# A graph-attention and quantile kernel: four engines ordered by hand in the attention, lists loaded one tile ahead, one product per half row of the search

## The chip, the core and the metric

The kernel runs on one core of one Trainium2 chip. A core has engines that work at the same time, each through its own list of instructions in order: TensorE (PE) for matrix products, VectorE (DVE), ScalarE (ACT) and GpSimd (POOL) for elementwise work, and SyncE (SP), which here issues DMA transfers only. ACT and POOL issue transfers too. Instructions of different engines wait for each other by semaphores. The metric is the device time of one execution in microseconds (us), lower is better, given as the median of several runs. A separate execution, recorded by the hardware profiler, gives the views that are read here.

## What is computed

Two graph layers over 4096 nodes with 128 features, both on the same adjacency matrix of integers (4096 x 4096, each entry 1 with chance 1/128, so some 32 neighbours a node). The first layer has eight heads (cut from the reference):

```python
Wh = jnp.einsum('nd,hde->hne', nodes, W)
f1 = jnp.einsum('hnd,hd->hn', Wh, a1)
f2 = jnp.einsum('hnd,hd->hn', Wh, a2)
e = jax.nn.leaky_relu(f1[:, :, None] + f2[:, None, :], negative_slope=ALPHA)
att = jnp.where((adj > 0)[None, :, :], e, jnp.float32(-9000000000000000.0))
att = jax.nn.softmax(att, axis=-1)
h = jax.nn.elu(jnp.einsum('hnm,hmd->hnd', att, Wh))
cat = jnp.transpose(h, (1, 0, 2)).reshape(N, NHEADS * DIM)
out = _layernorm(nodes + jax.nn.elu(cat @ W1 + b1), gamma, beta)
```

The second layer removes some neighbours of each node by their rank in its list, sorts the rest feature by feature, takes the mean of the three quartiles, mixes it with the node's own row, and multiplies by a last matrix:

```python
vals = jnp.where(keep[:, :, None], x[None, :, :], big)
svals = jnp.sort(vals, axis=1)
for q in QUANTILES:
    idx = jnp.maximum(jnp.ceil(q * n_keep).astype(jnp.int32) - 1, 0)
    picked = jnp.take_along_axis(svals, idx[:, None, None], axis=1)[:, 0, :]
    agg = agg + w_q * picked
agg = (1.0 - SELF_RATIO) * agg + SELF_RATIO * x
out = agg @ W.T + b + x
```

## The kernel before

Nodes are handled in tiles of 128, one node per partition, in three blocks of 2, 8 and 22 tiles (`BLOCKS`, L54). A block goes through these steps.

**Search** (`neighbours`, L532). For each tile the adjacency rows come in two halves of 2048 integers (1 MB, issued from ACT, three buffers `adj_t`). ACT turns a half into bf16 signs and counts them (L547). DVE then works in pieces: for 512 columns it multiplies the signs by a falling ramp `back` (L568), so that each entry holds its place in a chunk of 128, and MAX8 (L573) takes the eight largest of each chunk. After both halves, more rounds of MAX8 (L585, L587) pull the neighbour list out of the chunks. The function is a generator: every `yield` is a piece, and a tile has `PIECES` of them.

**Records and order** (`complete_records` L592, `rank_by_count` L652). A record holds a node's list, its number of neighbours, its own index, its scores and its features. The nodes of a block are ranked by their number of neighbours, and POOL scatters the records by rank to a DRAM tensor `recs_d` of that block (L379), one scatter per tile (`scatter`, L193, an indirect DMA). Tiles that are read back then have lists of similar length, so each has a fixed cap (`CAPS`).

**Attention on a sorted tile**, driven by `step` (L342):
- `fetch_rows` (L755) loads the records `R` back from SP (L762). Columns of the list come in layers 32, 32, 16, 8 or 4 wide (`layers`, L75). A layer narrower than 32 puts several nodes' neighbours in a row and loads list and scores again from SP (L771, L775), eight transfers a layer. DVE transposes lists and scores (L791 to L799) to `idx` and `f1x`. Then POOL gathers the neighbours' rows of `xt_d` one column at a time into `G` or, for a short rest, `Gs` (`gather`, L184, an indirect DMA of 128 rows).
- `weigh_rows` (L816), one tile later: DVE and ACT form scores and exponentials `z` (L825 to L827), DVE spreads them to `pf` (L839), PE sums weighted rows in PSUM tiles `y` (L860), ACT copies each `y` to `raw` (L871), DVE divides by the sum (L875 to L878), PE turns and ACT copies to `yT` (L887, L888).
- `transform` (L895), once for every two tiles, or four in the last block: the head matrices, ELU, `W1`, ELU and the layer norm, with the result `x1` (L954 to L974). `step` scatters `x1` to DRAM (L347, named x_d in the profile) at the following call.

`weigh_rows` and `transform` are generators too. `step` advances the weighing by a turn, then the open transform by a turn, then so many pieces of the next block's search; after the search's quota of the step it returns. In the first two blocks DVE, PE and ACT follow exactly this order (`manual_schedule(engines=ORDERED)`, L407), while POOL's order is left to a scheduler. In the last block, where no search is left, all are left to the scheduler. That block also ranks all 4096 nodes, scatters their lists to `all_d` (L397, four tiles a step), and works out kept neighbours and slots from it (`kept_rows`, `slot_places`). Three more calls of `step` (L414) finish the open tiles.

**Sort** (L424 to L470): POOL gathers the kept neighbours' `x1` rows (`vals`), DVE and ACT run a selection network on them (L1129, L1133), and the result is scattered to the output. Here all four engines have a hand order, which the change leaves alone.

Buffers come from pools with a fixed number each. `R` has 5 in the first two blocks and 8 in the last, `idx` and `f1x` 6, `sgn` 2, `y` 4 of one PSUM bank. `G` has 2, and a third in the last block (`take`, L744). A tile that is written waits until the readers of the buffer's earlier use are done.

Of the kernel before, what the change touches and what calls it, by code (L numbers as in the profile page):

```python
# [9 lines left out]
F32 = mybir.dt.float32  # L10
BF16 = mybir.dt.bfloat16
I32 = mybir.dt.int32
# [4 lines left out]
DRAM = bass.MemoryType.DRAM  # L17
ORDERED = {mybir.EngineType.DVE, mybir.EngineType.PE, mybir.EngineType.Activation}
ALL = ORDERED | {mybir.EngineType.Pool}

# [43 lines left out]
TURN = 12  # L64
YBANKS = 4

# [142 lines left out]
def kernel(  # L209
# [132 lines left out]
    def step(fetch=None, pieces=None, quota=0, size=2, more=None):  # L342
        if fetch:
            weigh.append(fetch_rows(tc, pools, narrow[turn[0] % 2], *fetch, xt_d, bad, uses))
            turn[0] += 1
        while store:
            scatter(nc, x1_d, *store.pop(0))  # L347
        if len(weigh) > 1 or (weigh and not fetch):
            R, parts = weigh.pop(0)
            place = len(members)  # L350
            members.append(R)
            turns = len(parts) + 13
            each = -(-quota // turns)
            done = 0
            for _ in weigh_rows(tc, attp, pools, pp, parts, turned, place, size, consts):
                if tails and next(tails[0], True):
                    tails.pop(0)
                for _ in range(min(each, quota - done)):
                    next(pieces, None)
                    done += 1  # L360
            quota -= done
            if len(members) == size:
                tails.append(
                    transform(tc, attp, pp, more, turned.pop(0), list(members), consts, store)
                )
                members.clear()
        elif not fetch:
            while tails:
                if next(tails[0], True):
                    tails.pop(0)  # L370
        for _ in range(quota):
            next(pieces, None)

    t0 = 0
    for b, n in enumerate(BLOCKS):
# [5 lines left out]
        if last:  # L381

            cp.release()
            adjp.release()
            wp = tc.alloc_tile_pool(name="order", bufs=1, side="right")
            cp = tc.alloc_tile_pool(name="cnt_all", bufs=2, side="right", reuse_waits="tile")
            found = rank_by_count(tc, cp, kp, num, jp1, before, oneb, 0, NT)
            ranks = wp.tile([P, NT], I32, name="ranks")
            nc.vector.tensor_copy(ranks, found)
            cp.release()  # L390
            cp = tc.alloc_tile_pool(name="lists", bufs=2, side="right", reuse_waits="tile")
            pools.append(cp)
            waiting = list(range(NT))
            for i in range(n):
                step((recs_d[b], i, CAPS[n][i], t0 + i), size=2 if i in (0, n - 1) else 4, more=kp)
                for t in waiting[:4]:
                    scatter(nc, all_d, rec[:, t, 0:REC1], ranks[:, t : t + 1])  # L397
                waiting = waiting[4:]
                if i == n // 2:
                    R = cp.tile([P, NT, REC1], F32, name="all", bufs=1)  # L400
                    nc.sync.dma_start(R, all_d.rearrange("(t p) w -> p t w", p=P))
                    kept_rows(tc, cp, R, jp1, pidx, idx, own_i, bad, limits)
                    slot_places(tc, cp, R, picks, limits)
        else:
            pieces = search(t0 + n, BLOCKS[b + 1])
            quota = -(-BLOCKS[b + 1] * PIECES // n)
            with tc.manual_schedule(engines=ORDERED):  # L407
                for i in range(n):
                    step((recs_d[b], i, CAPS[n][i], t0 + i), pieces, quota, more=kp)
                for _ in pieces:  # L410
                    pass
        t0 += n
    for _ in range(3):
        step(size=2, more=kp)  # L414
    count_bad(tc, cp, kp, bad, ones, total)
    cp.release()
# [115 lines left out]
def neighbours(tc, adjp, rec, num, adj, tiles, back, chunk):  # L532
# [11 lines left out]
    def sign():  # L544
        t, i, cnt, adj_t = loads.pop(0)
        sgn = adjp.tile([P, half], BF16, name="sgn", bufs=2)
        nc.scalar.activation(sgn, adj_t, AF.Sign, accum_out=cnt[:, i : i + 1])  # L547
# [6 lines left out]
    for _ in range(3):  # L554
        load(*todo.pop(0))
    sign()
    while signs:
        if loads:
# [4 lines left out]
        if i == 0:  # L563
            first = adjp.tile([P, NCH * 8], F32, name="first")
        for b in range(half // 512):

            key = sgn[:, ts(b, 512)].rearrange("p (c w) -> p c w", w=CW)
            nc.vector.tensor_tensor(  # L568
                key, key, back.unsqueeze(1).to_broadcast([P, 512 // CW, CW]), ALU.mult
            )  # L570
            c0 = i * half + b * 512
            for c in range(512 // CW):
                nc.vector.max(first[:, ts(c0 // CW + c, 8)], key[:, c, :])  # L573
            yield
# [17 lines left out]
def complete_records(tc, cp, rec, num_all, bad, jp1, pidx, t0, n):  # L592
# [3 lines left out]
    for a in range(t0, t0 + n, step):  # L596
# [11 lines left out]

        has = tmp("has")
        nc.vector.tensor_scalar(has, keys, 0.0, None, ALU.is_gt)  # L610
# [133 lines left out]
def take(pools, shape, name, turn, bufs=2):  # L744
# [3 lines left out]
    if len(pools) > 1:  # L748
        turn[name] = turn.get(name, 0) + 1
        if name == "R" or (name == "G" and turn[name] % 3 == 0):  # L750
            pool, bufs = pools[1], 8 if name == "R" else 1
    return pool.tile(shape, F32, name=name, bufs=bufs)


def fetch_rows(tc, ap, narrow, rec_d, i, cap, t, xt_d, bad, turn):  # L755

    nc = tc.nc

    R = take(ap, [P, REC], "R", turn, 5)
    rows = rec_d[ts(i, P), :]  # L760
# [19 lines left out]
    parts = []  # L780
    G, col = None, 0
    for s0, w in layers(cap):
        k = P // w
        idx = ap[0].tile([P, 32], I32, name="idx", bufs=6)
        if w == 32:
# [6 lines left out]
        if w < 32 or f1x32 is None:  # L792
# [4 lines left out]
            )  # L797
            f1x = ap[0].tile([P, 32 * H], F32, name="f1x", bufs=6)
            nc.vector.transpose(f1x, f1b.rearrange("p h g -> p (h g)"))  # L799
        if w == 32:  # L800
            f1x32 = f1x
        f1v = f1x.rearrange("p (h g) -> p g h", h=H)[:, 0:w, :]
        if w == 32:
            G, col = take(ap, [P, 32, XW], "G", turn), 0
# [11 lines left out]
def weigh_rows(tc, ap, pools, pp, parts, turned, place, size, consts):  # L816
# [16 lines left out]
    for half in range(2):  # L833
# [13 lines left out]
        for b in range(4):  # L847
            y = pp.tile([P, 512], F32, name="y", bufs=YBANKS)[:, 0 : 2 * (D + 1)]
            yv = y.rearrange("p (a d) -> p a d", a=2)
            for i, ((w, k, G, _), pf) in enumerate(zip(parts, pfs)):  # L850
                both = w == 32 or (w == 16 and split == 1)
                m = max(min(k * H, P) * (2 if both else 1), 32)
                for p0 in range(0, P, m):
# [4 lines left out]
                    else:  # L858
# [35 lines left out]

def transform(tc, ap, pp, more, yT, members, consts, store):  # L895

# [486 lines left out]
```

## Time and profile before

| what | us |
|---|---|
| median of 3 runs | 3860.11 |
| lowest and highest of them | 3859.21, 3861.66 |
| the profiled execution | 4473.73 |
| its span, first to last instruction | 4471.8 |
| DVE busy | 2634.2 |
| POOL busy | 2284.8 |
| ACT busy | 1265.3 |
| PE busy | 815.7 |

The stages of the profiled execution can be told by their transfers. The first search runs until the first records are scattered at 77 us. Block 0's attention and the search of the next 8 tiles take until 325, block 1's attention and the search of the last 22 tiles until 1101, where the records of the last block begin to be scattered. The last block gathers until 2412, its tail ends near 2487, where the sort's gathers begin, and the sort runs to the end.

A table of windows gives, for each stretch, the busy time and instructions of each engine. Busy time counts only what an engine does; POOL's issue of an indirect transfer counts[...], and the pause between two of them does not. A list of waits gives, for an engine and line, what its idle time waited for, in total, how often and at the longest. "issue" means that the profile shows nothing it waited for, "remote" a releaser that it can't name. A timeline line is one instruction or a run of equal ones: start, busy time, engine, line, operation and tiles, and in brackets the idle time before it with its releaser. The profiled execution is longer than the timed ones, so its times are not those of a timed run one by one.

### The profile page before, as it was taken

To read this page: it belongs to the slowest core of one execution; us is meant where nothing else is said; L and a number is where in the kernel's file an instruction comes from. 1 tells how busy PE (TensorE), PEld (TensorE's weight loads), DVE (VectorE), ACT (ScalarE), POOL (GpSimd) and SP (SyncE) were. 2 spreads that over 40 slices of the span, in tenths; PEclk is the share of its full clock that TensorE was granted. 3 is DMA by queue.
4 is the path that set the end of the run, shared out by engine and by line. 5 is a ranking of instruction groups with operands and counts; after the bars stand their busy time and mean duration, and the time that the engine had idled before them with its cause. 6 is when DMAs were issued, how large, how long until landed. Compare 5 with 4: busy or idle time off the path is not lost. (4 is left out here: it accounts for less than half of the span.)

```text
span 4471.8 us, 18412 instructions
## 1 busy us (share of the span) xinstructions
PE 815.7 (18%) x2751; PEld 469.4 (10%) x2753; DVE 2634.2 (59%) x5147; ACT 1265.3 (28%) x2352; POOL 2284.8 (51%) x2452
## 2 busy tenths in 40 slices
PE   2001212223231413332425110000000001000101
PEld 1000110111121201111112000000000000000001
DVE  5665667767111205110212436888878999999897
ACT  2112222222010213121213213333333444443433
POOL 1332343454657465756663575666565334455530
PEclk9955555555565656655656555555555555555555
DMA  5313333231222121212221111111111001111110
GB/s 168 105 48 111 97 101 96 91 93 43 54 46 53 36 57 41 55 47 48 48 51 28 40 53 39 47 45 47 40 45 41 22 21 30 31 38 35 36 28 3
DMA packets 115233, 241.18 MB, mean 54 GB/s; under 512 B 51904, under 2 KB 68288, under 8 KB 106912
## 3 DMA queue, kind: packets, MB, share of 16 engines
q0 software_dynamic: 76224, 161.01, 14.2%
q10 hardware_dynamic: 12160, 68.49, 4.5%
q1 hardware_dynamic: 26720, 10.41, 1.2%
q14 instruction: 103, 0.84, 0.1%
q8 instruction: 26, 0.43, 0.0%
HBM read 228.56 MB, written 11.18 MB: 54 GB/s over the span
## 5 line engine op out<-in xcount | busy, mean ns | idle before, releaser
L1133 DVE TENSOR_TENSOR vals<-low,vals 128x1024 f32<-128x1024 f32 (+9 forms) x1359 | 1403.0, 1058 | 338.9 <-ACT low L1129 129.8
L185 POOL DMA_INDIRECT G<-xt_d,idx x1092 | 1060.0, 971 | 736.3 <-issue 480.8
L185 POOL DMA_INDIRECT vals<-x_d,idx x960 | 911.9, 950 | 295.4 <-issue 287.5
L1129 ACT COPY low<-vals 128x1024 f32<-128x1024 f32 (+10 forms) x701 | 607.4, 876 | 968.6 <-DVE vals L1133 621.1
L871 ACT COPY raw<-y 32x129 f32<-32x129 f32 (+1 forms) x928 | 239.2, 258 | 854.6 <-remote 516.9
L860 PE MATMUL y<-G,pf 128*64 128x258 f32 (+1 forms) x1200 | 289.9, 518 | 978.3 <-issue 574.9
L1143 PE MATMUL st_ps<-ident,u 128*128 128x128 f32 x344 | 87.1, 437 | 1781.4 <-ACT u L1142 1377.9
L194 POOL DMA_INDIRECT out_dram<-o,own_i x32 | 31.8, 992 | 626.0 <-ACT o L1155 623.7
L875 DVE TENSOR_SCALAR rden<-raw 128x8 f32<-128x8 f32 x32 | 6.2, 194 | 550.5 <-ACT raw L871 407.0
L573 DVE MAX8 first<-sgn 128x8 f32<-128x128 bf16 x1024 | 223.9, 281 | 152.4 <-remote 121.5
L1143 PEld LDWEIGHTS st_ps<-ident,u 128*128 128x128 f32 x344 | 76.0, 327 | 1792.3 <-ACT u L1142 1385.4
L860 PEld LDWEIGHTS y<-G,pf 128*64 128x64 f32 (+1 forms) x1200 | 141.5, 191 | 1111.7 <-issue 861.6
L547 ACT ACTIVATE sgn<-adj_t 128x2048 bf16<-128x2048 int32 x64 | 122.1, 1907 | 303.0 <-DVE first L573 177.0
L908 DVE TENSOR_SCALAR e<-e 128x512 f32<-128x512 f32 x64 | 28.0, 437 | 242.4 <-ACT e L935 131.8
L194 POOL DMA_INDIRECT x_d<-x,R x32 | 32.9, 1027 | 260.2 <-DVE x L974 235.6
L888 ACT COPY yT<-turned 128x512 f32<-128x512 f32 x64 | 65.6, 1026 | 302.6 <-PE turned L887 157.2
L839 DVE TENSOR_TENSOR pf<-z,own 128x512 f32<-128x512 f32 x124 | 80.6, 683 | 112.1 <-issue 87.5
L887 PE MATMUL turned<-ident,raw 128*128 128x128 f32 x256 | 68.6, 420 | 391.6 <-DVE raw L878 233.1
L916 PE MATMUL o<-hv,W_sb 128*128 128x256 f32 (+1 forms) x176 | 93.8, 650 | 229.6 <-DVE hv L910 118.5
L1133 DVE TENSOR_TENSOR most<-low,most 128x1024 f32<-128x1024 f32 (+7 forms) x116 | 131.9, 1167 | 2.6 <-issue 0.5
L185 POOL DMA_INDIRECT Gs<-xt_d,idx x92 | 89.6, 974 | 85.7 <-remote 30.0
L585 DVE MAX8 rec<-first 128x8 f32<-128x256 f32 x256 | 109.3, 427 | 35.8 <-remote 18.7
(180 smaller groups left out, 1774.7 us busy)
## 6 DMA issues: line engine op xcount, KB each, us to landing
adj_t<-in_adj_dram ACTq DMA_DIRECT2D x64, 1024.0 KB
G<-xt_d,idx POOLq DMA_INDIRECT x1092
vals<-x_d,idx POOLq DMA_INDIRECT x960
R<-rec_d SPq DMA_DIRECT2D x128, 26.4 KB
xt_d<-rec SPq DMA_DIRECT2D x4, 548.0 KB
score<-rec_d SPq DMA_DIRECT2D x132, 1.0 KB
rec<-in_x_dram SPq DMA_DIRECT2D x4, 512.0 KB
Gs<-xt_d,idx POOLq DMA_INDIRECT x92
```

Of the source, the lines that this page charges most:

```text
L185: nc.gpsimd.indirect_dma_start(out=dst, out_offset=None, in_=rows, in_offset=bass.IndirectOffsetOnAxis(ap=idx, axis=0),)
L547: nc.scalar.activation(sgn, adj_t, AF.Sign, accum_out=cnt[:, i : i + 1])
L573: nc.vector.max(first[:, ts(c0 // CW + c, 8)], key[:, c, :])
L585: nc.vector.max(top, first)
L839: nc.vector.tensor_tensor(pf.rearrange("p (g k h) -> p g k h", g=g2, k=k), z[:, ts(half, g2), :].unsqueeze(2).to_broadcast(spread), own[w] ...
L860: nc.tensor.matmul(yv[p0 : p0 + m], lhsT=pf[:, c : c + m], rhs=rhs, start=(i == 0), stop=(i == len(parts) - 1), skip_group_check=True,)
L871: nc.scalar.copy(raw[p0 : p0 + m, 4 * half + b, :], yv[p0 : p0 + m, a, :])
L887: nc.tensor.transpose(t_ps[:, b, :], yn[:, 4 * half + b, :], ident)
L916: nc.tensor.matmul(o, lhsT=consts["W1_sb"][:, h, :], rhs=hv[:, ts(j, n)], start=(h == 0), stop=(h == H - 1),)
L1129: nc.scalar.copy(kept, low)
L1133: nc.vector.tensor_tensor(high if end else low, kept, high, ALU.max if end else ALU.min)
L1143: nc.tensor.matmul(st_ps, lhsT=u, rhs=ident, start=(i == 0), stop=(i == len(terms) - 1))
```

## The change

- All four engines (POOL too) follow a hand order in the attention of all three blocks; the three closing steps and the count of bad rows are moved into the last block's ordered region. `ORDERED` goes.
- `fetch_rows` is split. `list_rows` (the loads from SP and DVE's transposes) runs one tile ahead: tile i+1's before the step of tile i, so at the start of a block two tiles' lists come first. `R` goes to 7 and 9 buffers, `idx` and `f1x` to 9.
- The search multiplies a half row by `back` in one instruction of 2048 instead of four of 512. `sgn` has 3 buffers and two signs are made ahead.
- `y` becomes a tile of two banks, with 2 buffers; ACT copies two blocks at once, so 928 copies of 32x129 become 464 of 32x258, and a tile's weighing has four turns fewer. A transform of four tiles takes more turns than one weighing has then and ends in the next tile's, so its `x1` is scattered one step later. `x1` gets a tile of its own in another pool.
- A temporary of `complete_records` shares a buffer.

In the last block the written order makes POOL issue, step by step, a tile's gathers, then the `x1` scatters that are due (two or four), then four `all_d` scatters. All 22 record scatters come ahead of them.

```diff
...
         if fetch:
-            weigh.append(fetch_rows(tc, pools, narrow[turn[0] % 2], *fetch, xt_d, bad, uses))
-            turn[0] += 1
+            weigh.append(fetch_rows(tc, pools, fetch, xt_d, uses))
         while store:
...
             members.append(R)
-            turns = len(parts) + 13
+            turns = len(parts) + 9
             each = -(-quota // turns)
...
                 tails.append(
-                    transform(tc, attp, pp, more, turned.pop(0), list(members), consts, store)
+                    transform(tc, attp, pools[0 if size == 2 else -1], pp, more, turned.pop(0), list(members), consts, store)
                 )
...
             next(pieces, None)
+
+    def lists(b, i):
+        turn[0] += 1
+        t = sum(BLOCKS[:b]) + i
+        cap = CAPS[BLOCKS[b]][i]
+        return list_rows(tc, pools, narrow[turn[0] % 2], recs_d[b], i, cap, t, bad, uses)
...
             waiting = list(range(NT))
-            for i in range(n):
-                step((recs_d[b], i, CAPS[n][i], t0 + i), size=2 if i in (0, n - 1) else 4, more=kp)
-                for t in waiting[:4]:
-                    scatter(nc, all_d, rec[:, t, 0:REC1], ranks[:, t : t + 1])
-                waiting = waiting[4:]
-                if i == n // 2:
-                    R = cp.tile([P, NT, REC1], F32, name="all", bufs=1)
-                    nc.sync.dma_start(R, all_d.rearrange("(t p) w -> p t w", p=P))
-                    kept_rows(tc, cp, R, jp1, pidx, idx, own_i, bad, limits)
-                    slot_places(tc, cp, R, picks, limits)
+            with tc.manual_schedule(engines=ALL):
+                ready = [lists(b, 0)]
+                for i in range(n):
+                    if i + 1 < n:
+                        ready.append(lists(b, i + 1))
+                    step(ready.pop(0), size=2 if i in (0, n - 1) else 4, more=kp)
+                    for t in waiting[:4]:
+                        scatter(nc, all_d, rec[:, t, 0:REC1], ranks[:, t : t + 1])
+                    waiting = waiting[4:]
+                    if i == n // 2:
+                        R = cp.tile([P, NT, REC1], F32, name="all", bufs=1)
+                        nc.sync.dma_start(R, all_d.rearrange("(t p) w -> p t w", p=P))
+                        kept_rows(tc, cp, R, jp1, pidx, idx, own_i, bad, limits)
+                        slot_places(tc, cp, R, picks, limits)
+                for _ in range(3):
+                    step(size=2, more=kp)
+                count_bad(tc, cp, kp, bad, ones, total)
         else:
...
             quota = -(-BLOCKS[b + 1] * PIECES // n)
-            with tc.manual_schedule(engines=ORDERED):
+            with tc.manual_schedule(engines=ALL):
+                ready = [lists(b, 0)]
                 for i in range(n):
-                    step((recs_d[b], i, CAPS[n][i], t0 + i), pieces, quota, more=kp)
+                    if i + 1 < n:
+                        ready.append(lists(b, i + 1))
+                    step(ready.pop(0), pieces, quota, more=kp)
                 for _ in pieces:
...
         t0 += n
-    for _ in range(3):
-        step(size=2, more=kp)
-    count_bad(tc, cp, kp, bad, ones, total)
     cp.release()
...
         t, i, cnt, adj_t = loads.pop(0)
-        sgn = adjp.tile([P, half], BF16, name="sgn", bufs=2)
+        sgn = adjp.tile([P, half], BF16, name="sgn", bufs=3)
         nc.scalar.activation(sgn, adj_t, AF.Sign, accum_out=cnt[:, i : i + 1])
...
     sign()
+    if loads:
+        sign()
     while signs:
...
             first = adjp.tile([P, NCH * 8], F32, name="first")
+        key = sgn.rearrange("p (c w) -> p c w", w=CW)
+        nc.vector.tensor_tensor(
+            key, key, back.unsqueeze(1).to_broadcast([P, half // CW, CW]), ALU.mult
+        )
         for b in range(half // 512):
...
-            key = sgn[:, ts(b, 512)].rearrange("p (c w) -> p c w", w=CW)
-            nc.vector.tensor_tensor(
-                key, key, back.unsqueeze(1).to_broadcast([P, 512 // CW, CW]), ALU.mult
-            )
             c0 = i * half + b * 512
             for c in range(512 // CW):
-                nc.vector.max(first[:, ts(c0 // CW + c, 8)], key[:, c, :])
+                nc.vector.max(first[:, ts(c0 // CW + c, 8)], key[:, b * (512 // CW) + c, :])
             yield
...
-        has = tmp("has")
+        has = tmp("c")
         nc.vector.tensor_scalar(has, keys, 0.0, None, ALU.is_gt)
...
         if name == "R" or (name == "G" and turn[name] % 3 == 0):
-            pool, bufs = pools[1], 8 if name == "R" else 1
+            pool, bufs = pools[1], 9 if name == "R" else 1
     return pool.tile(shape, F32, name=name, bufs=bufs)
...
-def fetch_rows(tc, ap, narrow, rec_d, i, cap, t, xt_d, bad, turn):
-
-    nc = tc.nc
-
-    R = take(ap, [P, REC], "R", turn, 5)
+def list_rows(tc, ap, narrow, rec_d, i, cap, t, bad, turn):
+
+    nc = tc.nc
+
+    R = take(ap, [P, REC], "R", turn, 7)
     rows = rec_d[ts(i, P), :]
...
     parts = []
-    G, col = None, 0
     for s0, w in layers(cap):
-        k = P // w
-        idx = ap[0].tile([P, 32], I32, name="idx", bufs=6)
+        idx = ap[0].tile([P, 32], I32, name="idx", bufs=9)
         if w == 32:
...
             )
-            f1x = ap[0].tile([P, 32 * H], F32, name="f1x", bufs=6)
+            f1x = ap[0].tile([P, 32 * H], F32, name="f1x", bufs=9)
             nc.vector.transpose(f1x, f1b.rearrange("p h g -> p (h g)"))
...
         f1v = f1x.rearrange("p (h g) -> p g h", h=H)[:, 0:w, :]
+        parts.append((s0, w, idx, f1v))
+    return R, cap, parts
+
+
+def fetch_rows(tc, ap, lists, xt_d, turn):
+
+
+    nc = tc.nc
+    R, cap, todo = lists
+    parts = []
+    G, col = None, 0
+    for s0, w, idx, f1v in todo:
+        k = P // w
         if w == 32:
...
         for b in range(4):
-            y = pp.tile([P, 512], F32, name="y", bufs=YBANKS)[:, 0 : 2 * (D + 1)]
-            yv = y.rearrange("p (a d) -> p a d", a=2)
+            if b % 2 == 0:
+                y = pp.tile([P, 2, 512], F32, name="y", bufs=2)
+            yv = y[:, b % 2, 0 : 2 * (D + 1)].rearrange("p (a d) -> p a d", a=2)
             for i, ((w, k, G, _), pf) in enumerate(zip(parts, pfs)):
...
                     )
+            if b % 2 == 0:
+                continue
             m = P // (2 * split)
             for p0 in range(0, P, m):
-                a = p0 // m % 2
-                nc.scalar.copy(raw[p0 : p0 + m, 4 * half + b, :], yv[p0 : p0 + m, a, :])
+                a = p0 // m % 2 * (D + 1)
+                nc.scalar.copy(
+                    raw[p0 : p0 + m, 4 * half + b - 1 : 4 * half + b + 1, :],
+                    y[p0 : p0 + m, :, a : a + D + 1],
+                )
             yield
...
-def transform(tc, ap, pp, more, yT, members, consts, store):
+def transform(tc, ap, own, pp, more, yT, members, consts, store):
...
     yield
-    x1 = ap.tile([P, 4, D], F32, name="x1", bufs=1)[:, 0:m, :]
+    x1 = own.tile([P, m, D], F32, name=f"x1_{m}", bufs=1)
     stats = ap.tile([P, 4, 6], F32, name="stats")
```

More of the change, by code (lines that the diff above doesn't have):

```diff
@@ L17 @@
 DRAM = bass.MemoryType.DRAM
-ORDERED = {mybir.EngineType.DVE, mybir.EngineType.PE, mybir.EngineType.Activation}
-ALL = ORDERED | {mybir.EngineType.Pool}
+ALL = {
+    mybir.EngineType.DVE,
+    mybir.EngineType.PE,
+    mybir.EngineType.Activation,
+    mybir.EngineType.Pool,
+}
 P = 128
@@ L64 @@
 TURN = 12
-YBANKS = 4
 R_NUM, R_OWN, R_F1 = L, L + 1, L + 2
```

## The prediction

> **What bounds the kernel now.** I read the span first, then a table of busy time by stage (cut where the record scatters, the last gather and the sort begin), then the waits of the engine that is busiest in each stage, and last single stretches of the timeline. Columns of the table: stage, length, busy us (instructions) of PE, weight loads, DVE, ACT, POOL, then clock and DMA.
>
> ```profile
> 77.00:325.00 248.00, 17.94 (x58) 7.49 (x59) 159.90 (x593) 38.79 (x64) 97.50 (x102) 0.79 0.32 88
> 325.00:1101.00 776.00, 180.82 (x593) 99.82 (x595) 505.96 (x1788) 192.15 (x393) 321.61 (x324) 0.57 0.30 91
> 1101.00:2412.00 1311.00, 402.63 (x1287) 196.56 (x1285) 255.47 (x668) 246.32 (x735) 820.12 (x848) 0.60 0.21 48
> ```
>
> To be seen: while blocks 0 and 1 run, DVE is the busiest engine (it does the neighbour search); in the last block (third row) DVE has 255 us of work in 1311 and POOL has 820 plus its dispatch. So a saving on DVE counts before 1101 us only, a saving or a loss on POOL after it only.
>
> POOL's row understates it. In the last block it issues gathers like this, and scatters to one DRAM tensor behind each other like the first four lines (start, duration, idle before and its releaser):
>
> ```profile
> 1165.92 0.96 POOL L194 DMA_INDIRECT all_d<-rec,ranks  x1 [0.30 <-issue]
> 1168.39 0.96 POOL L194 DMA_INDIRECT all_d<-rec,ranks  x1 [1.51 <-DMA all_d<-rec,ranks]
> 1171.01 0.95 POOL L194 DMA_INDIRECT all_d<-rec,ranks  x1 [1.66 <-DMA all_d<-rec,ranks]
> 1173.47 0.96 POOL L194 DMA_INDIRECT all_d<-rec,ranks  x1 [1.51 <-DMA all_d<-rec,ranks]
> 1174.74 0.97 POOL L185 DMA_INDIRECT G<-xt_d,idx  x1 [0.30 <-issue]
> 1176.02 0.96 POOL L185 DMA_INDIRECT G<-xt_d,idx  x1 [0.30 <-issue]
> ```
>
> A gather takes 1.25 us from start to start (2405.01 to 2411.25: five in 6.24). A scatter behind a scatter takes 2.52 (1165.92 to 1173.47: three in 7.55), 1.27 more, because it waits until the one before has landed; a single one between gathers takes 1.27 in all.
>
> What stands idle in the two stages beside that (engine, what waited, for whom: us, times, longest):
>
> ```profile
> DVE first L573 <- remote: 121.5, 28, 5.9
> DVE bad L776 <- DMA R<-rec_d: 42.5, 2, 25.4
> DVE z L825 <- DMA G<-xt_d,idx: 34.3, 3, 19.7
> ...
> DVE idx L791 <- DMA list<-rec_d: 7.7, 4, 2.9
> ```
>
> ```profile
> POOL G L185 <- issue: 247.7, 702, 16.3
> POOL x_d L194 <- DVE x L974: 53.3, 2, 44.1
> POOL G L185 <- PE y L860: 47.0, 3, 17.0
> POOL Gs L185 <- remote: 29.7, 3, 16.3
> POOL Gs L185 <- PE y L860: 29.5, 2, 18.3
> ```
>
> Without the 0.30 that belongs to each dispatch, POOL's idle in the last block adds to about 211 us. **The choice that decides this forecast is how much of it exists in a timed run.** The profiled execution took 4473.7 us (span 4471.8), 612 more than the median 3860.1. Much of its idle has no cause that it shows: DVE's own MAX8 waits 4.3 us (121.5/28) behind a product of the same engine. Floor: up to 1101, DVE's "remote" and "issue" waits sum to about 190, leaving 911. The last block without POOL's idle is 1311 - 211 = 1100; its tail 75. The sort (2487 to 4472) is 1985; DVE waits 129.8 there for ACT's copy L1129, 94.8 on "issue" and 30.2 on "remote", leaving 1730. Sum 3816: 44 us under the median, where 656 us of such idle were taken out. So a timed run seems to hold at most about 44 of the last block's 211, by an even share 14. I take 25.
>
> [...] 128x1024 bf16 in 0.68 us, 128x1920 in 1.15. [...] L568 takes 0.41 us for 512 where the fp32 L839 takes 0.68[...].
>
> **The change part by part.**
>
> One product per half row. A piece (product of 512 and four MAX8) repeats every 1.23 us: products start at 800.03 and 801.26. A half row is four, 4.94. After: one product of 2048, by the two bf16 rows above 1.15 + 128 x 0.525 ns = 1.21, plus 16 MAX8 at 0.193 to 0.212, 3.1: 4.33. Saved 0.61 x 60 half rows = 37 us on DVE while it bounds (the first four half rows lie in the opening search, which waits for loads). It also cuts product-to-MAX8 waits from 256 to 64; should a share of the 121.5 us be real (44/656 of it, three quarters gone), 6 more. Together -43; bounds -20 and -90. A third `sgn` buffer and the second sign ahead mean a load is issued after an earlier sign: one load in flight less, +3 in the opening (bounds 0 and +6), nothing later, where a half row comes every 15 us or slower[...].
>
> Lists one tile ahead. What goes: DVE's list waits, 7.7, and the later of the two `R` waits, 17 (42.5 - 25.4), of which I take 10. What comes: at the start of a block SP issues tile 1's lists before tile 0 is weighed, 28 issues at 0.30 to 0.42 for a tile with three narrow layers, +9 at block 1, where the first `R` wait of 25.4 stays. Net -1.
>
> The border to the last block. Before, the last tile of block 1 is weighed around 1098.58, where DVE waits 7.6 us for its gathers and the first record scatter stands behind two x1 scatters that end at 1101; its last needed rank stood at 1089.66. After, that weigh is ordered behind the lists of tiles 0 and 1 and the record scatters start earlier: -8. But the first gather of the last block writes a `G` that this weigh still reads. Before, from first record scatter to first gather: 1101.3 to 1174.7, 73.4, with 17 of the 32 all_d scatters in the waits between record scatters. After: 22 record scatters alone, 62; lists of tile 0 from SP, then of tile 1, about 11 each (1167.2 to 1175.5), and the DVE transposes behind them; then z, exp, pf and the matmuls, 13.6 as at 1098.6 to 1112.2: about 101. +27 on POOL (bounds +10 and +40).
>
> Scatters in bunches. By POOL's order after, all_d goes in fours behind each tile's gathers and x1 in fours or twos before: 35 scatters have a scatter to the same tensor ahead. 35 x 1.27 = 45. Besides, 17 all_d and 2 x1 scatters leave the shadow of the record scatters, where they cost nothing: 19 x 1.26 = 24. +69, less what falls where POOL would wait for a buffer anyway (bounds +40 and +80).
>
> POOL, PE, ACT and DVE by hand in the last block. The number of gathers, 776, is the same: 969 us at 1.25 cannot be ordered away. What can go is idle: -25 as chosen, bounds 0 and -211. The x1 scatters one tile later take away the 44.1 wait for `x`; in that count already. The `R` buffers (9) let a list load wait for an x1 scatter two steps back; three `G` buffers cover it, 0.
>
> Copies of two blocks at once. ACT: 928 copies at 0.268 become 464 at about 0.38 (0.258 plus 129 elements at 0.87 ns, from 128x512 in 0.596 and 128x128 in 0.263): -70 on ACT, which is busy 246 of 1311 us. Nothing, hidden by POOL's gathers; a `y` freed later costs PE a block, hidden too. Uncovered it would be up to 1 us a half tile. The sort is untouched: 0.
>
> Sum: -43 + 3 - 1 - 8 + 27 + 69 - 25 = +22. Most of the profiled excess should come again, so the sum is laid on the median: 3860 + 22 = 3882.
>
> **The rivals.** (1) The idle is real: if the sort and the search hold none of it and gathers run quicker unprofiled, the last block could lose 100 or more. Hand order then removes the waits for `x` (53.3), for `y` (76.5) and remote (29.7). It turns the result once more than 47 us go. With 110: 3860 + 47 - 110 = 3797. For it: the same waits end after PE's `y` on buffers, a plain cause. Against: the floor of 3816. (2) The bunches fall into existing waits: half of the 69 and 12 of the 27 vanish: 3882 - 46 = 3836, also faster. (3) Even: product and idle weigh against the border and bunches, about 3860. (4) The product of 2048 loses the double rate: 2048 x 1.04 ns + 0.15 = 2.3 us (fp32 rows: 512 in 0.68, 1024 in 1.21), 1.1 more each, so 0.49 lost instead of 0.61 saved, 66 us worse: 3948. Against: the 512 row keeps it with the same kind of view.
>
> **How the numbers follow.** A median of this kernel can be told from no change at about 0.2%, 8 us. Forecast 0.43; rival 1 0.26; rival 2 0.18; even 0.10; rival 4 0.03. Faster 0.44, same 0.10, slower 0.46. The predicted time is that of the likeliest case, 3882; its own range, with product -20 to -50, bunches 40 to 80, border 10 to 40 and idle 0 to 44, is 3850 to 3925. To hold 8 in 10 it reaches to rivals 1 and 2: 3790 to 3925.
>
> **What would show it.** Product: 64 rows of 128x2048 near 1.2 us, and the record scatters of the last block starting some 50 us earlier. Border: about 100 us from first record scatter to first gather instead of 73. Bunches: all_d in fours 2.5 us apart. If between the first and the last gather POOL's idle falls far below 211 and the timed run falls with it, the floor was wrong; if it falls and the time doesn't, the idle was the profile's. It is wrong altogether if POOL shows new waits for `R`, `idx` or `G` inside the stream.

## The result and the profile after

The changed kernel takes 3893.8 us (median of 4 runs, 3892.2 to 3897.4), the kernel before 3860.0 beside it: a ratio of 1.0089, 95% interval 1.0075 to 1.0103. It is slower by 34 us, where 22 were forecast.

The profile of the kernel before that the prediction reads (4473.7 us), and the first group of experiments below, are from executions in which the unchanged kernel takes some 4400 to 4470 us instead of 3860. Each group of experiments ran on one chip, a different one each time, and all executions of the unchanged kernel in a group lie at one level: 23 near 4435 in the first, 25 and 7 near 3860 in the others. So times are compared only within a group, or by their ratios to the kernel before. The profile after lies at the usual level (span 3893.3), and a second profile of the kernel before was taken there (span 3853.1, the run `e10_before_again`). These two can be set side by side.

Busy time by stage of the kernel after, in the columns of the prediction's table. The cuts are again the first record scatters of blocks 0, 1 and 2, and the last gather:

```profile
74.60:256.90 182.30, 18.62 (x58) 7.69 (x59) 152.74 (x552) 34.35 (x46) 103.70 (x102) 0.83 0.44 122
256.90:814.00 557.10, 167.53 (x574) 94.85 (x575) 479.20 (x1637) 173.28 (x271) 343.05 (x322) 0.60 0.41 126
814.00:2021.10 1207.10, 376.61 (x1375) 197.59 (x1375) 285.90 (x700) 215.89 (x465) 825.64 (x850) 0.62 0.23 52
```

The same of the kernel before, second profile:

```profile
76.50:263.30 186.80, 18.16 (x59) 7.44 (x59) 158.72 (x596) 38.79 (x64) 99.45 (x103) 0.82 0.41 117
263.30:873.45 610.15, 176.27 (x595) 98.97 (x596) 506.17 (x1786) 191.98 (x393) 323.83 (x325) 0.60 0.37 115
873.45:1984.80 1111.35, 398.86 (x1372) 204.38 (x1370) 273.74 (x703) 264.39 (x778) 826.53 (x848) 0.65 0.22 57
```

To be seen: the two search stages are 57.6 us shorter (4.5 and 53.1), and the last block is 95.8 longer with the same POOL work (825.6 against 826.5 busy). So POOL waits more.

POOL's waits from the first to the last gather of the last block, before (second profile), then from its first record scatter on, after:

```profile
POOL G L185 <- issue: 206.7, 678, 0.3
POOL Gs L185 <- issue: 17.7, 58, 0.3
POOL G L185 <- DMA G<-xt_d,idx: 6.1, 20, 0.3
POOL x_d L194 <- issue: 5.4, 14, 1.4
...
POOL x_d L194 <- DVE wt L1103: 1.7, 1, 1.7
```

```profile
POOL G L188 <- issue: 213.2, 694, 1.4
POOL all_d L197 <- DMA all_d<-rec,ranks: 38.1, 24, 2.7
POOL rec_d L197 <- DMA rec_d<-rec,ranks: 37.5, 20, 2.4
POOL G L188 <- PE y L889: 35.9, 5, 34.6
...
POOL x_d L197 <- DMA x_d<-x,R: 12.9, 8, 1.9
```

Before, every wait in this stream is the 0.3 of a dispatch, but for a few of under 2 us (3.7 us in all beyond the dispatches): there is next to no idle that an order could remove. After, one gather waits 34.6 us, and 24 `all_d` scatters wait for the one ahead to land. On the timeline 14 `x1` scatters stand directly behind another and wait as long; the list gives the scatter ahead as the cause for 8 of them only. Beyond the 0.30 of a dispatch these 38 waits sum to 52.3 us. A bunch of each kind, and that gather, on POOL's timeline:

```profile
945.40 0.96 POOL L197 DMA_INDIRECT all_d<-rec,ranks  x1 [0.30 <-issue]
947.84 0.96 POOL L197 DMA_INDIRECT all_d<-rec,ranks  x1 [1.48 <-DMA all_d<-rec,ranks]
950.31 0.96 POOL L197 DMA_INDIRECT all_d<-rec,ranks  x1 [1.52 <-DMA all_d<-rec,ranks]
952.76 0.96 POOL L197 DMA_INDIRECT all_d<-rec,ranks  x1 [1.49 <-DMA all_d<-rec,ranks]
...
1276.94 1.00 POOL L197 DMA_INDIRECT x_d<-x,R  x1 [0.30 <-issue]
1279.47 0.97 POOL L197 DMA_INDIRECT x_d<-x,R  x1 [1.53 <-DMA x_d<-x,R]
1282.75 1.00 POOL L197 DMA_INDIRECT x_d<-x,R  x1 [2.31 <-DMA R<-rec_d]
1285.59 1.40 POOL L197 DMA_INDIRECT x_d<-x,R  x1 [1.84 <-DMA x_d<-x,R]
```

```profile
910.82 0.97 POOL L188 DMA_INDIRECT G<-xt_d,idx  x1 [34.65 <-PE y L889]
```

The last record scatter starts at 875.22. On DVE meanwhile (kernel after) the lists of tiles 0 and 1 come first, and the weighing whose `G` is wanted starts only at 899.40:

```profile
881.07 0.15 DVE L793 TENSOR_SCALAR bad<-R 128x1 f32<-128x1 f32 x1 [51.39 <-DMA R<-rec_d]
...
889.42 0.15 DVE L793 TENSOR_SCALAR bad<-R 128x1 f32<-128x1 f32 x1 [1.28 <-DMA R<-rec_d]
...
899.40 0.59 DVE L853 TENSOR_TENSOR z<-G,f1x 128x256 f32<-128x256 f32 x1
```

The stages of all kernels, worked out from POOL's timelines (us): when the last block's first record scatter starts, and from there how long it is to the first gather, from that to the end of the last gather, to the sort's first gather, and to the end. The column of gathers holds 776 gathers in every kernel, and the scatters between them: 808 transfers in all before, 828 after.

| kernel | record scatters | to first gather | gathers | tail | sort | span |
|---|---|---|---|---|---|---|
| before, second profile | 873.5 | 73.9 | 1037.5 | 43.2 | 1825.0 | 3853.1 |
| after | 814.0 | 96.8 | 1110.3 | 47.3 | 1824.9 | 3893.3 |
| after less before | -59.4 | +22.9 | +72.8 | +4.1 | -0.1 | +40.2 |
| e9_product_again | 842.9 | 72.3 | 1036.2 | 43.2 | 1825.7 | 3820.3 |
| e5_after_again | 814.7 | 98.1 | 1111.8 | 46.8 | 1825.9 | 3897.3 |
| e6_border | 851.1 | 78.5 | 1106.1 | 47.0 | 1825.4 | 3908.0 |
| e7_singles | 815.3 | 98.4 | 1058.8 | 48.5 | 1825.4 | 3846.3 |
| e8_all_three | 861.6 | 74.6 | 1045.4 | 48.7 | 1825.3 | 3855.6 |
| e11_ordered_border | 809.5 | 71.7 | 1057.6 | 48.0 | 1824.9 | 3811.8 |
| e12_ordered_all | 812.0 | 69.3 | 1051.2 | 47.6 | 1825.8 | 3805.8 |
| first group: e1_before_again | 1083.3 | 74.5 | 1197.1 | 75.6 | 1977.0 | 4407.5 |
| e2_product_only | 976.6 | 73.9 | 1219.4 | 75.6 | 1978.1 | 4323.6 |
| e3_after_four_products | 1098.7 | 99.1 | 1201.2 | 83.8 | 1978.9 | 4461.7 |
| e4_copies_only | 1085.9 | 75.7 | 1195.0 | 84.0 | 1977.5 | 4418.2 |

The profiled executions are 40.2 apart, the medians 34 (39 in the second group below); single executions scatter by a few us.

### The profile page after: what moved, and what is told of

The parts are those of the page before. It is cut to its first block, busy times and chain, and to the rows that moved or that the text cites. A ratio compares the mean times of both kernels' runs of the same rounds, so it can differ in the third digit from the quotient of the medians.

```text
span 3893.3 us, 17676 instructions
## 1 busy us (share of the span) xinstructions
PE 747.3 (19%) x2751; PEld 449.7 (12%) x2753; DVE 2621.1 (67%) x4955; ACT 1196.5 (31%) x1888; POOL 2317.4 (60%) x2452
## 5 line engine op out<-in xcount | busy, mean ns | idle before, releaser
L188 POOL DMA_INDIRECT G<-xt_d,idx x1092 | 1092.0, 1000 | 510.2 <-issue 323.3
L889 PE MATMUL y<-G,pf 128*64 128x258 f32 (+1 forms) x1200 | 255.7, 492 | 907.7 <-DVE pf L867 867.1
L853 DVE TENSOR_TENSOR z<-G,f1x 128x256 f32<-128x256 f32 (+3 forms) x46 | 22.1, 479 | 463.6 <-DMA G<-xt_d,idx 461.6
L855 ACT ACTIVATE z<-z 128x256 f32<-128x256 f32 (+3 forms) x62 | 20.4, 330 | 878.9 <-DVE z L854 877.7
L902 ACT COPY raw<-y 32x258 f32<-32x258 f32 (+1 forms) x464 | 169.7, 366 | 252.8 <-PE y L889 217.2
L590 DVE MAX8 first<-sgn 128x8 f32<-128x128 bf16 x1024 | 208.1, 277 | 2.0
L1167 DVE TENSOR_TENSOR vals<-vals 128x256 f32<-128x256 f32 (+2 forms) x335 | 119.0, 411 | 0.0
L950 PE MATMUL o<-hv,W_sb 128*128 128x256 f32 (+1 forms) x176 | 81.6, 579 | 187.7 <-DVE hv L944 187.7
L197 POOL DMA_INDIRECT rec_d<-rec,ranks x32 | 31.2, 976 | 129.5 <-DVE rec L528 67.2
```

Of the source, the lines that this page charges most:

```text
L188: nc.gpsimd.indirect_dma_start(out=dst, out_offset=None, in_=rows, in_offset=bass.IndirectOffsetOnAxis(ap=idx, axis=0),)
L197: return nc.gpsimd.indirect_dma_start(out=rows, out_offset=bass.IndirectOffsetOnAxis(ap=idx, axis=0), in_=src, in_offset=None,)
L590: nc.vector.max(first[:, ts(c0 // CW + c, 8)], key[:, b * (512 // CW) + c, :])
L889: nc.tensor.matmul(yv[p0 : p0 + m], lhsT=pf[:, c : c + m], rhs=rhs, start=(i == 0), stop=(i == len(parts) - 1), skip_group_check=True,)
L902: nc.scalar.copy(raw[p0 : p0 + m, 4 * half + b - 1 : 4 * half + b + 1, :], y[p0 : p0 + m, :, a : a + D + 1],)
L950: nc.tensor.matmul(o, lhsT=consts["W1_sb"][:, h, :], rhs=hv[:, ts(j, n)], start=(h == 0), stop=(h == H - 1),)
```

## The experiments

The theory is that of the prediction: the product and the lists save time while DVE bounds; the border and the bunches lose it on POOL, which has little or nothing to give in the last block. The rivals: the idle of the last block is real, so that the hand order removes it (the first of the prediction) or the bunches fall into it (the second); the product is hidden, or takes 2.3 us instead of 1.21.

**First group: parts alone.** The kernel before takes 4434.8 us in it.

Unchanged, for a profile (`e1_before_again`):

> The kernel before, unchanged, for a second profile. My theory: the 612 us that its first profile had above the median were the profile's own, so a fresh profile near 3860 us has its stages as follows: record scatters of the last block begin near 860 (the changed kernel: 814), first gather about 73 us later, last gather near 2000, sort about 1825 long as in the changed kernel, and POOL idle in the last block under 45 us. Rival (the idle is real): the record scatters begin earlier than 840 and over 60 us of POOL idle that no scatter explains stand between the first and the last gather. If the profile is again near 4470, neither is told apart.

4409.4 us: at the longer level again, so nothing is told apart. POOL still has long waits in its gathers there (`Gs` for PE's `y` up to 18.4 us), and the stretch takes 1197.1 instead of 1037.5.

Product alone (`e2_product_only`), in the kernel before:

```diff
-        for b in range(half // 512):
-            key = sgn[:, ts(b, 512)].rearrange("p (c w) -> p c w", w=CW)
-            nc.vector.tensor_tensor(key, key, back...to_broadcast([P, 512 // CW, CW]), ALU.mult)
+        key = sgn.rearrange("p (c w) -> p c w", w=CW)
+        nc.vector.tensor_tensor(key, key, back...to_broadcast([P, half // CW, CW]), ALU.mult)
+        for b in range(half // 512):
```

> The kernel before with one product of 2048 per half row, all else as before. My theory: DVE bounds up to the last block, so 60 half rows save 0.61 us each and 0 to 6 us of waits: -37 to -43, 3817 to 3823. Rival A: the product is hidden by other waits, 3850 to 3860. Rival B: the product loses the double rate, about 3888.

4320.5 us, ratio 0.9749 (0.9718 to 0.9779): 114 us, three times the expectation. A product of 2048 takes 1.209 us here, not the 2.3 that rival B means. The two profiles, 83.9 us apart, show where it comes from. MAX8 of the kernel before, then with one product (busy, mean ns, idle before and its releasers):

```profile
L573 DVE MAX8 first<-sgn 128x8 f32<-128x128 bf16 x1024 | 223.8, 281 | 143.4 <-remote 97.0 <-issue 35.6 <-DVE sgn L568 4.1
```

```profile
L573 DVE MAX8 first<-sgn 128x8 f32<-128x128 bf16 x1024 | 209.7, 278 | 22.8 <-issue 12.2 <-remote 5.7 <-DVE sgn L566 3.1
```

At this level the idle before MAX8 falls by 120.6 us with one product; at the usual level the same group has 7.9 us of idle before the change, and no more can go. So the 114 don't carry over.

The changed kernel with four products (`e3_after_four_products`; the edit is the reverse of the one above):

> The changed kernel with four products of 512 per half row again, all else changed. My theory: 37 to 43 us slower than the changed kernel's 3894, 3931 to 3937, if DVE bounds the search there too. Rival: in the changed kernel POOL's gathers of block 1 end no earlier than DVE's ranks, so part of the product's gain is lost already: 3905 to 3920.

4463.8 us, 1.0083 (1.0051 to 1.0115) of the kernel before. The changed kernel itself isn't in this group, so the size asked for stays open. What the table shows: the wait at the border is there again (99.1 against 74.5), while the gathers take only 4.1 us longer than in `e1_before_again`. By POOL's timelines 38 scatters in bunches wait 54.7 us beyond their dispatches there, and the waits ahead of gathers fall from 143.7 to 91.0. So at the level where POOL has idle in its stream, its loss pays for the bunches. Whether the bunches fall into it, as the second rival said, or the hand order removes it, as the first said, isn't told apart.

Copies of two blocks alone (`e4_copies_only`), in the kernel before:

```diff
-            y = pp.tile([P, 512], F32, name="y", bufs=YBANKS)[:, 0 : 2 * (D + 1)]
+            if b % 2 == 0:
+                y = pp.tile([P, 2, 512], F32, name="y", bufs=2)
...
-                nc.scalar.copy(raw[p0 : p0 + m, 4 * half + b, :], yv[p0 : p0 + m, a, :])
+                nc.scalar.copy(raw[p0 : p0 + m, 4 * half + b - 1 : 4 * half + b + 1, :], y[p0 : p0 + m, :, a : a + D + 1])
```

> The kernel before with y in tiles of two banks and ACT's copies of two blocks at once, all else as before (the weighing has as many turns as before). My theory: ACT is not the bound in any stage, 3855 to 3862. Rival: the later release of y or the later end of a weighing holds DVE in block 1 or POOL in the last block: 3865 to 3885; or the fewer ACT instructions free DVE, 3835 to 3850.

4424.4 us, 0.9984 (0.9969 to 0.9998), next to nothing, as said. A copy of 32x258 takes 365 ns in the kernel after, one of 32x129 takes 257 in the kernel before.

**Second group: the border and the bunches in the changed kernel.** The kernel before takes 3860.3 us here, and the changed one first, as the reference (`e5_after_again`):

> The changed kernel once more, as the reference of this group. If the kernel before runs near 3860 here: 3885 to 3900. If it runs near 4435 as in the last group, there the change's product is worth 114 us instead of 37 and the changed kernel should be faster than before: 4464 - 114 to 4464 - 60, 4350 to 4404, with the same costs of border and bunches in it.

3899.0 us, 1.0102 (1.0085 to 1.0119).

The border (`e6_border`):

```diff
             with tc.manual_schedule(engines=ALL):
+                step(size=2, more=kp)
                 ready = [lists(b, 0)]
```

> The changed kernel, but in the last block the last tile of block 1 is weighed ahead of the lists of tiles 0 and 1 instead of behind them. My theory: the first gather no longer waits for the G of that tile and follows the record scatters by about 12 us instead of 35: -20 to -27 against the changed kernel, about the same on either kind of chip. Rival: POOL gets ahead and waits as long for G later in the stream, or the weighing moved forward delays the lists: 0 to -5.

3908.6 us, 10 slower than the changed kernel: a miss. The wait before the first gather did go (78.5 from the first record scatter instead of 98.1), but the record scatters themselves start 36 us later. The weighing came ahead of the last search tile and of the ranks on DVE: the ranking isn't part of the hand-ordered region, and the scheduler put it behind the weighing's start. DVE then sits on the gathers, and POOL on the ranks:

```profile
827.62 0.60 DVE L854 TENSOR_TENSOR z<-G,f1x 128x256 f32<-128x256 f32 x1 [26.65 <-DMA G<-xt_d,idx]
```

```profile
851.12 0.96 POOL L197 DMA_INDIRECT rec_d<-rec,ranks  x1 [10.72 <-DVE ranks L734]
```

Single scatters (`e7_singles`); `between` holds the step's four `all_d` scatters and the `x1` scatters that are due:

```diff
         for g in range(w):
             gather(nc, G[:, col + g, :], xt_d, idx[:, g : g + 1])
+            if g % 3 == 2 and between:
+                scatter(nc, *between.pop(0))
...
-                    for t in waiting[:4]:
-                        scatter(nc, all_d, rec[:, t, 0:REC1], ranks[:, t : t + 1])
```

> The changed kernel, but in the last block all_d and x1 scatters go one by one behind every third gather instead of in fours and twos. My theory: each scatter that had one of its tensor ahead saves 1.27 us, 32 or so of them: -35 to -45 against the changed kernel. Rival (the bunches fall where POOL would wait for G anyway, as PE or DVE set its pace): -10 or less, with new waits for y in their place.

3846.7 us, 52 less than the changed kernel, and 0.9964 (0.9951 to 0.9976) of the kernel before. That is more than the 35 to 45 expected, and what the 38 waits of the kernel after sum to. The gathers take 1058.8 us instead of 1110.3 to 1111.8, and no new wait for `y` comes. The rival falls. POOL's timeline of it; behind the first gather one scatter waits 1.1 us, and no other longer than a dispatch:

```profile
922.01 0.94 POOL L188 DMA_INDIRECT G<-xt_d,idx  x1 [0.30 <-issue]
923.26 1.00 POOL L197 DMA_INDIRECT all_d<-rec,ranks  x1 [0.30 <-issue]
924.56 0.96 POOL L188 DMA_INDIRECT G<-xt_d,idx  x1 [0.31 <-issue]
```

Both, with eight `all_d` scatters between the last eight record scatters (`e8_all_three`). The block's ranks are first copied to a tile that outlives their pool:

```diff
+                for i in range(14, n):
+                    scatter(nc, all_d, rec[:, waiting[0], 0:REC1], ranks[:, waiting[0] : waiting[0] + 1])
+                    waiting.pop(0)
+                    scatter(nc, recs_d[b], rec[:, t0 + i, :], held_i[:, i : i + 1])
```

> The changed kernel with both: the border mended, single scatters, and besides eight of the all_d scatters put between the last eight record scatters, where those wait anyway. My theory: -24 - 40 - 10 = -65 to -85 against the changed kernel, so faster than both kernels: 3810 to 3830 where the kernel before takes 3860. Rival: POOL's gain is eaten by waits for G (PE y), -20 to -40.

3853.2 us, 46 less than the changed kernel but 7 more than with single scatters alone. Neither account: no wait for `G` took the gain. The failure of `e6_border` is in it, with the first record scatter at 861.6, where POOL had waited 33.7 us for a copy of the ranks.

**Third group.** The kernel before takes 3857.7 us.

Product alone again (`e9_product_again`):

> The kernel before with one product of 2048 per half row, once more, for a chip on which the kernel before takes 3860. My theory: -37 to -43 there, 3817 to 3823; its profile shows record scatters of the last block from about 820 and POOL idle in the last block, beside the 0.30 of each dispatch and scatter waits, under 45 us. Rival (the product is worth what it was in the slower group, 114 us): 3746. Rival (most of it is hidden): 3850 or more.

3828.1 us, 0.9925 (0.9908 to 0.9941): 29.6 us, less than the 37 to 43 expected. The record scatters start 30.6 us earlier than before (842.9, not 820), and everything behind them is as it was.

The kernel before again (`e10_before_again`):

> The kernel before for a second profile, on a chip where it takes 3860. My theory: record scatters of the last block from about 860, first gather 73 us later, last gather near 1985, POOL's idle in the last block under 45 us where the first profile had 211. Rival: idle over 60 us there, so that the hand order did remove something.

3855.0 us. Scatters from 873.5 (860 expected), first gather 73.9 later, last gather ending at 1984.8. The waits shown above leave 3.7 us of idle among the gathers of the last block: the first rival falls at this level.

The border in another way (`e11_ordered_border`), on top of the single scatters:

```diff
-            found = rank_by_count(tc, cp, kp, num, jp1, before, oneb, 0, NT)
...
             with tc.manual_schedule(engines=ALL):
+                found = rank_by_count(tc, cp, kp, num, jp1, before, oneb, 0, NT)
...
+                early = list(store)
+                store.clear()
+                step(size=2, more=kp)
+                store[0:0] = early
                 ready = [lists(b, 0)]
```

> The changed kernel with single scatters (3847 as measured), and the border mended in another way than in the run that failed: the ranking of all nodes also stands in the hand-ordered region, so that the weighing of block 1's last tile is ordered behind all ranks and ahead of the lists, and the x1 scatters that were ready go between the next gathers. My theory: the first gather follows the record scatters by about 12 us, -20 to -25 against 3847: 3820 to 3827. Rival (the border is not worth it: ranks or lists become late instead): 3842 or more.

3818.4 us, 0.9901 (0.9884 to 0.9917). Against `e7_singles`, by their ratios to the kernel before: 0.0063 x 3860 = 24 us, by their intervals within 8 us or so. The first gather follows the first record scatter by 71.7 instead of 98.4, and waits now for its own lists only:

```profile
871.28 0.96 POOL L197 DMA_INDIRECT rec_d<-rec,ranks  x1 [1.98 <-DMA rec_d<-rec,ranks]
881.20 0.97 POOL L188 DMA_INDIRECT G<-xt_d,idx  x1 [8.95 <-DVE f1b L814]
```

With eight `all_d` scatters among the record scatters (`e12_ordered_all`):

> The same with eight all_d scatters between the last eight record scatters besides. My theory: eight scatters of 1.26 us leave the stream, -6 to -10 against the run before, 3810 to 3820, and faster than both kernels. Rival: the record scatters are delayed by as much, no difference.

3807.6 us, 0.9869 (0.9852 to 0.9885): 50 us faster than the kernel before and, by the ratios, 85 to 90 than the changed one. The step from `e11_ordered_border` is 10.7 (the profiled executions are 6.0 apart). POOL's timeline shows how it comes: the 22 record scatters keep their pace, 59.6 us from the first to the last instead of 61.8, and the others stand in their waits.

```profile
852.19 0.96 POOL L198 DMA_INDIRECT rec_d<-rec,picks  x1 [1.87 <-DMA rec_d<-rec,picks]
853.45 0.96 POOL L198 DMA_INDIRECT all_d<-rec,ranks  x1 [0.30 <-issue]
854.90 0.96 POOL L198 DMA_INDIRECT rec_d<-rec,picks  x1 [0.48 <-DMA rec_d<-rec,picks]
856.16 0.96 POOL L198 DMA_INDIRECT all_d<-rec,ranks  x1 [0.30 <-issue]
```

## Why the prediction was right, and its terms that were mis-sized

The way it goes and the two causes of the loss are as forecast. That the sum came within 12 us of the median is in part luck: two terms were each over 20 us off, in opposite directions. The sign that would have made it wrong altogether, new waits for `R`, `idx` or `G` inside the stream, didn't appear: behind the first gather of the last block the other gathers wait 1.7 us in all beyond their dispatches. By its own steps:

- **The product** (-43, of it -37 for the work and -6 for waits): shown, mis-sized. `e9_product_again` measures -29.6. The product in it, and MAX8 in the kernel before at the same level:

```profile
L566 DVE TENSOR_TENSOR sgn<-sgn,back 128x2048 bf16<-128x2048 bf16 x64 | 77.3, 1209 | 9.6 <-ACT sgn L547 9.6
```

```profile
L573 DVE MAX8 first<-sgn 128x8 f32<-128x128 bf16 x1024 | 223.7, 280 | 7.9
```

  A product of 2048 takes 1.209 us (forecast 1.21), and a half row runs from 319.13 to 323.49 on DVE, 4.36 (forecast 4.33). The price of a half row was right; 60 of them at 4.94 - 4.36 make 35, of which some 4 don't reach the record scatters. The 6 for waits was no gain beside it: the idle before MAX8 falls from 7.9 to 1.9 us at this level, some 0.03 a product, and that lies inside the half rows as they were timed.
- **Lists ahead and the border's weighing moved behind the ranks** (-1, -8 and +3 in the opening: -6): mis-sized. The record scatters start 28.8 us earlier after the change than with the product alone. DVE's waits for gathers up to there, with the product alone and after, are the largest difference of the two lists:

```profile
DVE z L825 <- DMA G<-xt_d,idx: 40.9, 4, 20.0
```

```profile
DVE sgn L583 <- ACT sgn L562: 19.3, 2, 10.1
...
DVE z L853 <- DMA G<-xt_d,idx: 4.9, 2, 4.1
```

  36 us go there, and some 10 come back as a wait for signs (9.6 with the product alone). On DVE's timeline the last of the four waits, 7.6 us, is the one at the border, priced as -8; two inside block 1, of 20.0 and 9.4, are gone as well. The prediction had this row in its own view (34.3, 3 times) and gave no price to the rest of it. That the lists' lead is the cause of the rest is argued from the rows; it wasn't tried alone. A rival stands beside it: with the product alone POOL stops in block 1 for `x1` scatters whose `x` DVE has yet to finish (18.0 us in 3 waits), and after the change, where POOL's order is written too, none of these waits is left.
- **The border** (+27): +22.9 measured; taking it away (`e11_ordered_border`) gives 24 by the ratios and 26.7 in its own stretch. Shown.
- **The bunches** (+69, as 45 and 24): +72.8 for the whole stretch of gathers. Taking the bunches apart gives 52 of it, and the waits themselves sum to 52.3: 38 scatters stand behind one to the same tensor where the prediction counted 35, and wait 1.38 us each beyond a dispatch instead of 1.27. With single scatters 21.3 us over the kernel before are left. They are the 20 scatters more that the stretch holds: 16 `all_d` and 4 `x1`, where the prediction counted 17 and 2 (between its record scatters stand 12 `all_d`, behind the last the four of its first view). Putting eight back gave 10.7. Shown, and close.
- **Idle that goes in the last block** (-25): nothing, at most the 3.7 us that were there. This is the other mis-sized term. The floor said at most 44 of the 211 were real, and a share of 14; the second profile says next to none. Without this term the forecast would have been +47 in all. Its error and that of the lists nearly cancel: -59.4 against -49 up to the border, +72.8 against +44 after it.
- **The copies**: nothing measurable, shown at the longer level. **The sort**: 0.1 us apart. **The tail**: 4.1 longer, where 0 was said. At the longer level the copies alone lengthen it, from 75.6 to 84.0, and one product leaves it at 75.6; so the copies are the likely cause, not tried alone at the usual level.
- **The rivals**: idle that pays for the bunches, as the first two have it, exists at the longer level (`e3_after_four_products`), not where the times were taken. That the product runs like the two bf16 rows of the prediction was the author's estimate from them, and it held: 1.209 us for 2048, after 0.409 for 512, is 0.52 ns for each element more, where the fp32 rows of L839 (512 in 0.683) and L878 (1024 in 1.222) in the kernel before grow by 1.05. This is the double rate that the fourth rival would have lost; it falls.

What stays open: why the same program has two levels, 3860 and 4435 us, and how the 28.8 us ahead of the record scatters divide between the lists' lead, POOL's order and the fewer turns of a weighing.

## What to carry to other kernels

A hand order can win what the engine that bounds the stage waits for. Where its waits are all dispatch, as POOL's were in the last block (3.7 us beyond it), there is nothing to win, and here the order lost by putting scatters to the same tensor next to each other (38 waits of 1.38 us each beyond a dispatch). One by one between gathers they cost a dispatch of 0.30 and their own 1.00 us (`e7_singles`), and in the waits of scatters to another tensor next to nothing: in `e12_ordered_all` the 22 record scatters take 59.6 us with eight `all_d` scatters among them, in `e11_ordered_border` 61.8 without. Here the first alone turned a loss of 1% into a gain of 0.4%. Before hiding a wait behind other work, look at what is queued behind that work on the same engine, and at which part of the program the hand order doesn't bind, as the first try at the border showed.

## What the runs showed of the hardware that was not expected

- The unchanged kernel takes 3855 to 3864 us in all executions of two groups and 4407 to 4446 in all of the first. Each group had a chip of its own, none was used twice, so whether the chip or the occasion makes the level is open. The granted clock is only some 2% lower (0.572 to 0.577 against 0.585 to 0.593). At the longer level the operations looked at take no longer (MAX8 281 against 280 ns, gathers still 1.25 us apart), but idle appears ahead of them, even behind products of the same engine: 143.4 against 7.9 us in the 1024 MAX8. The sort takes 1977 instead of 1825. So one product in place of four was worth more there: 114 us against 29.6.
- The name of a releaser can mislead where an instruction waits for several things. The gather at the border waits 34.65 us for "PE y" in the kernel after and 34.95 for "DMA R" with single scatters, in the same place. The lists of its tile were done at 888.1 in the kernel after, 23 us ahead of it, and moving the weighing ahead of the lists (`e11_ordered_border`) left a wait of 8.95 for lists, so it was PE.
